# Two steps a unit and a fixed order for TensorE in one stage of a decoder kernel on Trainium2

## The chip, the cores and the metric

The kernel runs on one core of a Trainium2 chip (trn2). TensorE (PE in the profile) multiplies and transposes into PSUM; VectorE (DVE), ScalarE (ACT) and GpSimd (POOL) do the rest; SyncE (SP) issues most DMAs. The metric is the device time of one execution in microseconds (us), as the median of several runs. A profile comes from one execution of its own.

## The reference, cut to what matters

Two decoder layers run over eight sequences of 512 tokens of width 256, all in fp32. The stage in question is the self-attention of layer 1:

```
def _L1_attn_ref(x, wq, w_kv_down, w_k_up, w_v_up, wo):      # x: 8 x 512 x 256
    H, D = 16, 64
    q = heads(x @ wq.T)                                       # 8, 16, 512, 64
    kv_latent = x @ w_kv_down.T                               # width 128
    k = heads(kv_latent @ w_k_up.T)
    v = heads(kv_latent @ w_v_up.T)
    q = q * cos + rotate_half(q) * sin
    k = k * cos + rotate_half(k) * sin
    scores = einsum('bhsd,bhtd->bhst', q, k) / sqrt(D) + causal
    probs = softmax(scores)
    out = einsum('bhst,bhtd->bhsd', probs, v)
    return merged(out) @ wo.T
x = layernorm(x + _L1_attn_ref(x, ...))
```

Ahead of it stand layer 0's self-attention, a cross-attention and a feed-forward block; behind it a joint attention over the sequence and a context, and a mixture of experts.

## The kernel before, in words

The stage `l1_self` goes through 64 units: a unit is one sequence b (a "batch" below, of eight units) and one pair of heads c. The causal mask makes the rows of queries of unequal length, so a unit's four row blocks i are put in three groups: `GROUPS = ((0, 1), (2,), (3,))`, which need 128 + 256, 384 and 512 columns of scores. The helper `_pipeline` (L32) walks over (b, c, group) and calls, at each step, the stages of different units: `l1_pre` and `l1_scores` for the newest, `l1_transposes` two steps later (there is an empty stage between) and `l1_values` three steps later. After each step it runs one piece of work that was put off: half of a batch's output projection.

What each stage does:

- `l1_prepare` cuts the projections into pieces. `share` (once a batch) transposes x (L198) and makes the latents (L844). `q_and_k` makes queries (L852) and keys (L853) in one PSUM tile of the kind `s`; VectorE multiplies it by the cosines into `qk` (L857) and by the sines into `turned` (L858), and four DMAs on POOL's queue add `turned`, with halves of heads exchanged, into `qk` (L861). `v` makes the values (L868), which ScalarE copies (L870). The pieces lie in one list, `ahead`, and `l1_pre` takes one at two of the three steps of a unit.
- `l1_scores` multiplies queries by keys (L907) into an `s` tile; the two heads use half of the array's rows each. `masked_softmax` adds the mask and takes the maximum on VectorE in one instruction (L271), negates and scales the maximum (L281), and takes the exponential with its sum on ScalarE (L283). `scaled` divides by the sum on VectorE (L891, L893).
- `l1_transposes` turns the probabilities on TensorE (L939), three or four blocks into a PSUM tile of the kind `t`, and `evac` copies it to SBUF: in turn on VectorE (L108) and on ScalarE (L110).
- `l1_values` multiplies values by turned probabilities (L963) into an `o` tile; the two heads use half of the array's columns each. After a unit's last group, `out_done` copies the tile out; after a batch's last unit it puts off the output projection (`project_and_norm`: L239, then the sum and the layer norm on VectorE, L246 and L213 to L223, with one instruction on POOL, L216).

The program order is not the order of execution: a scheduler orders each engine's instructions at compile time by priority (the place in the program) and by when its own model thinks that operands and buffers are ready. In `l1_self` this holds for all engines. The next stage, `l1_context`, keeps TensorE in program order (`tc.manual_schedule(engines={PE})`). A tile that asks for a buffer in use makes its first writer wait.

[...] The setting `psum("b", 2, 2, 2)` gives two `s` tiles [...], two `t` tiles and two `o` tiles; `psum("c", 2, 3, 1)`, opened for the next stage, gives two, three and one. Under the latter, tiles made by `u_tile` come from `t`.

## Time and profile before

| What | Value |
|---|---|
| Median of 3 runs | 3648.78 us (3641.66 to 3656.81) |
| The profiled execution: its own time, its span | 3650.17 us, 3648.5 us |
| Busy share of the span: PE, DVE, ACT, POOL | 94%, 60%, 39%, 30% |
| Mean granted TensorE clock | 0.965 |
| Stage `l1_self`: first latents to last output projection | about 1257 to 2206 us |

A line of groups reads: line, engine, operation, tile written <- tiles read, shape, count, busy time and mean duration, and the idle time of the engine before it with what ended it. A line of waits reads: who waited <- for whom: us in total, times, longest. A line of stretches reads: from:to, length, busy time and count of PE, PEld, DVE, ACT and POOL, then the granted clock (1.00 is full), the share of the DMA engines, and GB/s. A line of the timeline reads: start, length, engine, line, operation, tiles, shape and count, and in brackets the idle time before it. A matrix product in fp32 leaves two records. For TensorE the first part of a shape, as 64*128, is the part of the array in use: rows and columns.

### The profile page before, as it was taken

Reading aid. Unit: us, or ns where it says so; the run is one execution under the profiler, and the core shown is the slowest. Engines: PE = TensorE matmul, PEld = TensorE weight load, DVE = VectorE, ACT = ScalarE, POOL = GpSimd, SP = SyncE. Lnnn points to the kernel's source line nnn. Section 1 sums busy time; section 2 is a strip of 40 time slices with the busy share of each in tenths; the row PEclk is TensorE's granted clock in tenths of the full one; section 3 lists DMA queues with packets and bytes.
Section 4 is the critical chain, followed back from the end, with each engine's and each line's share of the span. In section 5 each row is a group of like instructions: output and inputs, shape, how many; then the busy total and the mean of one; then the engine's idle time right before and its main releaser. Section 6 shows DMA issues by size and latency. Waiting matters only on the chain. (4 is left out here: it accounts for less than half of the span.)

```text
span 3648.5 us, 52874 instructions
## 1 busy us (share of the span) xinstructions
PE 3429.4 (94%) x19718; PEld 2117.7 (58%) x19718; DVE 2173.6 (60%) x6158; ACT 1437.9 (39%) x2947; POOL 1092.5 (30%) x960
## 2 busy tenths in 40 slices
PE   8999999998999899999999999999999998999995
PEld 3333343345666556665666666555555555888884
DVE  5776776656666377778777885665666655200112
ACT  2444444453434254445444553433333333222222
POOL 3877777762111122222222220010101101222222
PEclk8999999998999999999999999999999999999997
DMA  4000011110000297232222330000000002766674
GB/s 132 30 24 24 24 36 33 38 60 12 4 1 1 52 270 165 36 41 36 36 36 36 41 47 4 10 13 18 20 8 21 19 13 92 230 179 190 184 229 134
DMA packets 166002, 234.97 MB, mean 64 GB/s; under 512 B 26569, under 2 KB 128649, under 8 KB 165746
## 3 DMA queue, kind: packets, MB, share of 16 engines
q1 hardware_dynamic: 139010, 175.83, 15.8%
q0 software_dynamic: 25584, 51.57, 9.4%
q8 instruction: 156, 2.56, 0.3%
q10 hardware_dynamic: 1152, 4.19, 0.3%
q14 instruction: 100, 0.82, 0.1%
HBM read 135.83 MB, written 61.11 MB: 54 GB/s over the span
## 5 line engine op out<-in xcount | busy, mean ns | idle before, releaser
L430 DVE CUSTOM_DVE_ANT_0 scored<-s_sc,decay 128x512 f32<-128x512 f32 x512 | 323.5, 687 | 221.7 <-PE s_sc L425 220.6
L861 POOL DMA_DIRECT2D qk<-turned x256 | 202.9, 1205 | 657.0 <-PE t_v L868 264.9
L483 ACT ACTIVATE pt<-s_st 128x1024 f32<-128x1024 f32 x256 | 261.1, 1023 | 262.1 <-PE s_st L479 232.9
L283 ACT ACTIVATE p<-p,nm 128x128 f32<-128x128 f32 (+3 forms) x512 | 283.1, 554 | 159.7 <-DVE nm L281 157.0
L110 ACT COPY pt<-tP 128x512 f32<-128x512 f32 (+2 forms) x416 | 205.6, 496 | 308.4 <-PE tP L939 189.4
L1082 ACT ACTIVATE p<-s_sc,nm 128x576 f32<-128x576 f32 x256 | 191.1, 747 | 342.7 <-DVE nm L1081 241.3
L893 DVE TENSOR_SCALAR p<-p,rsum 128x576 f32<-128x576 f32 (+4 forms) x768 | 295.8, 427 | 5.5
L1439 DVE TENSOR_SCALAR y<-o_y,share 128x256 f32<-128x256 f32 x71 | 31.4, 479 | 397.2 <-PE o_y L1419 397.2
L1402 PE MATMUL s_h<-xnT,we 128*128 128x256 f32 (+1 forms) x1248 | 262.1, 364 | 0.6 <-DMA we<-in_mo_w 0.6
L1081 DVE TENSOR_REDUCE nm<-s_sc 128x1 f32<-128x576 f32 x256 | 185.2, 748 | 115.4 <-PE s_sc L1079 114.0
L1419 PE MATMUL o_y<-we,h 128*128 128x256 f32 x1136 | 251.4, 379 | 0.0
L271 DVE CUSTOM_DVE_ANT_0 p<-s_sc,tabs 128x128 f32<-128x128 f32 (+3 forms) x512 | 232.6, 482 | 16.5 <-PE s_sc L907 16.5
L108 DVE COPY pt<-tP 128x512 f32<-128x512 f32 (+2 forms) x416 | 235.9, 576 | 8.0 <-PE tP L1097 3.6
L1402 PEld LDWEIGHTS s_h<-xnT,we 128*128 128x128 f32 x1248 | 218.0, 192 | 25.5 <-DMA we<-in_mo_w 1.0
L1419 PEld LDWEIGHTS o_y<-we,h 128*128 128x128 f32 x1136 | 215.3, 190 | 29.0
L1440 POOL DMA_INDIRECT total<-y,to x71 | 110.2, 1553 | 397.8 <-DVE y L1439 181.7
L907 PE MATMUL s_sc<-qk 64*128 64x128 f32 (+3 forms) x1024 | 205.8, 474 | 14.3 <-DMA qk<-turned 12.7
L939 PEld LDWEIGHTS tP<-ident,p 128*128 128x128 f32 x1280 | 136.6, 140 | 126.2 <-issue 58.4
L939 PE MATMUL tP<-ident,p 128*128 128x128 f32 x1280 | 192.5, 283 | 11.8 <-DVE pt L108 8.0
L425 PE MATMUL s_sc<-k,q 32*128 32x512 f32 x1024 | 174.5, 671 | 25.8 <-ACT pt L483 23.2
L1245 POOL DMA_INDIRECT rows_in<-z,irow x64 | 62.8, 982 | 415.4 <-DVE hit L1240 304.8
L963 PE MATMUL o_pv<-pt,vc 128*64 128x128 f32 (+1 forms) x2304 | 184.2, 293 | 0.0
(282 smaller groups left out, 6566.4 us busy)
## 6 DMA issues: line engine op xcount, KB each, us to landing
we<-in_mo_w SPq DMA_DIRECT2D x78, 1024.0 KB, 5.7
rows_in<-zero SPq DMA_DIRECT2D x64, 530.0 KB, 12.8
qk<-turned POOLq DMA_DIRECT2D x256, 128.0 KB, 4.5
coef<-in_ff_upw SPq DMA_DIRECT2D x40, 256.0 KB, 3.2
coef<-in_ff_dnw SPq DMA_DIRECT2D x40, 256.0 KB, 3.2
xr<-rows_in SPq DMA_DIRECT2D x32, 265.0 KB, 6.4
x<-in_x SPq DMA_DIRECT2D x8, 512.0 KB, 9.8
total<-x SPq DMA_DIRECT2D x8, 512.0 KB, 2.9
```

The costliest lines, as they stand in the source:

```text
L108: dve.tensor_copy(dst, src)
L110: act.copy(dst, src)
L271: dve.tensor_tensor_reduce(out=p[:, j, 0:n], in0=s[:, j, 0:n], in1=m, scale=1.0, scalar=-3.0e38, op0=op, op1=reduced, accum_out=mx[:, j : ...
L283: act.activation(p[:, j, 0:n], p[:, j, 0:n], AF.Exp, bias=nm[:, j : j + 1], scale=scale, accum_out=sums[:, at + j : at + j + 1],)
L430: dve.tensor_tensor_reduce(out=scored[:, h, :], in0=s[:, j, :], in1=decay[:, i, :], scale=1.0, scalar=-3.0e38, op0=ALU.mult, op1=ALU.max, ...
L483: act.activation(pt, s, AF.Exp, scale=1.0 / 16.0)
L861: pool.dma_start(out=qk[h : h + 32], in_=other[g : g + 32], accum_op=ALU.add)
L893: dve.tensor_scalar(p[:, j, 0:n], p[:, j, 0:n], rsum[:, j : j + 1], None, ALU.mult)
L907: pe.matmul(s[:, j, at : at + n], lhsT=q[h : h + 64, i * P : (i + 1) * P], rhs=k[h : h + 64, 0:n], start=True, stop=True,)
L939: pe.transpose(t[:, n, :], p[:, j, at * P : (at + 1) * P], ident)
L1402: pe.matmul(s[:, j, :], lhsT=w1[:, c, f * P : (f + 1) * P], rhs=xnT[:, c, :], start=(c == 0), stop=(c == KC - 1),)
L1419: pe.matmul(o[:, i, :], lhsT=h[:, f, i * P : (i + 1) * P], rhs=w2[:, f, :], start=(f == 0), stop=(f == 7),)
```

## The change

1. A unit has two steps instead of three: group 0, then groups 1 and 2 together (`STEPS`). Each stage runs for all groups of its step. The transposes follow one step after the scores and the values two steps after, with no empty stage.
2. TensorE runs the stage in program order.
3. Queries and keys are projected two units ahead, with a third `qk` buffer; values one unit ahead. The transposes of x and the latents of the next batch are separate pieces at the two steps of unit 5. Before the loop come unit 0's pieces and unit 1's queries and keys.
4. In `masked_softmax` the VectorE instruction scales by -1/8 and takes the minimum, which gives the negated scaled maximum directly: the separate negation is gone, and the exponential's scale is -1.
5. The transposed probabilities are copied by ScalarE alone, into three buffers instead of two.
6. The PSUM setting `c` is opened before the stage instead of after it.

```diff
-    def masked_softmax(s, p, m, n, scale, add_or_mult, sums, at):
-
-        mx = col("mx", 2)
+    def masked_softmax(s, p, m, n, scale, sums, at):
+
         nm = col("nm", 2)
-        op, reduced = add_or_mult
         for j in range(2):
+
             dve.tensor_tensor_reduce(
                 out=p[:, j, 0:n],
                 in0=s[:, j, 0:n],
                 in1=m,
-                scale=1.0,
-                scalar=-3.0e38,
-                op0=op,
-                op1=reduced,
-                accum_out=mx[:, j : j + 1],
+                scale=-scale,
+                scalar=3.0e38,
+                op0=ALU.add,
+                op1=ALU.min,
+                accum_out=nm[:, j : j + 1],
             )
-        dve.tensor_scalar(nm, mx, -scale, None, ALU.mult)
         for j in range(2):
             act.activation(
                 p[:, j, 0:n], p[:, j, 0:n], AF.Exp,
-                bias=nm[:, j : j + 1], scale=scale, accum_out=sums[:, at + j : at + j + 1],
+                bias=nm[:, j : j + 1], scale=-1.0, accum_out=sums[:, at + j : at + j + 1],
             )
...
+    banks.close()
+    ctx.enter_context(psum("c", 2, 3, 1))
+
     def l1_prepare(b, c):
...
-        def share():
-            xT = x_transposed(b)
+        def turn():
+            live["xT", b] = x_transposed(b)
+
+        def latent():
+            xT = live["xT", b]
             latT = work.tile([P, S], F32, tag="lat", name="lat")
-            o = o_tile("o_lat")
+            o = u_tile("o_lat")
...
-            qk = ph.tile([P, 2, S], F32, tag="qk", name="qk", bufs=2)
+            qk = ph.tile([P, 2, S], F32, tag="qk", name="qk", bufs=3)
...
-        return ([share] if c == 0 else []) + [q_and_k, v]
-
-    ahead = [piece for b in range(NB) for c in range(8) for piece in l1_prepare(b, c)]
+        return ([turn, latent] if c == 0 else []) + [q_and_k, v]
+
+    units = [(b, c) for b in range(NB) for c in range(8)]
+    pieces_of = {u: l1_prepare(*u) for u in units}
 
     GROUPS = ((0, 1), (2,), (3,))
 
-    def l1_pre(b, c, m):
-
-        if (b, c, m) == (0, 0, 0):
-            for _ in range(3):
-                ahead.pop(0)()
-        if ahead and (m or c == 7):
-            ahead.pop(0)()
+    STEPS = ((0,), (1, 2))
+
+    def l1_pre(b, c, step):
+
+        at = units.index((b, c))
+        if step == 0 and at + 2 < len(units):
+            pieces_of[units[at + 2]].pop(-2)()
+        if step == 1 and at + 1 < len(units):
+            pieces_of[units[at + 1]].pop()()
+        if c == 5 and b + 1 < NB:
+            pieces_of[b + 1, 0].pop(0)()
...
+    def groups(stage):
+
+
+        def run(b, c, step):
+            for m in STEPS[step]:
+                stage(b, c, m)
+
+        return run
...
-        pt = pt_tile()
+        pt = pt_tile(bufs=3)
         order = [at for block in l1_blocks(m) for _, at in block]
         for j in range(2):
             t = t_tile("tP")
             for n, at in enumerate(order):
                 pe.transpose(t[:, n, :], p[:, j, at * P : (at + 1) * P], ident)
-            evac(pt[:, j, 0 : len(order), :], t[:, 0 : len(order), :])
+            act.copy(pt[:, j, 0 : len(order), :], t[:, 0 : len(order), :])
...
-    with phase("l1_self") as ph:
+    with phase("l1_self") as ph, tc.manual_schedule(engines={PE}):
+        for u, what in ((0, 0), (0, 0), (0, 0), (0, 0), (1, 0)):
+            pieces_of[units[u]].pop(what)()
         _pipeline(
-            [(b, c, m) for b in range(NB) for c in range(8) for m in range(len(GROUPS))],
-            [l1_pre, l1_scores, nothing, l1_transposes, l1_values],
+            [(b, c, step) for b in range(NB) for c in range(8) for step in range(len(STEPS))],
+            [
+                (0, groups(l1_scores)),
+                (0, l1_pre),
+                (1, groups(l1_transposes)),
+                (2, groups(l1_values)),
+            ],
             put_off,
         )
```

More of the change, by code (lines that the diff above doesn't have):

```diff
@@ L257, in p_tile, with pt_tile @@
         return ph.tile([P, 2, n], F32, tag="p", name="p", bufs=bufs)
-    def pt_tile():
-        return ph.tile([P, 2, NT, P], F32, tag="pt", name="pt")
+    def pt_tile(bufs=2):
+        return ph.tile([P, 2, NT, P], F32, tag="pt", name="pt", bufs=bufs)
     def col(name, n):
         return work.tile([P, n], F32, tag=name, name=name, bufs=4)
-    def masked_softmax(s, p, m, n, scale, add_or_mult, sums, at):
-        mx = col("mx", 2)
+    def masked_softmax(s, p, m, n, scale, sums, at):
         nm = col("nm", 2)
-        op, reduced = add_or_mult
         for j in range(2):
@@ L845, in share @@
             evac(latT, o)
-            live["xT", b], live["lat", b] = xT, latT
+            live["lat", b] = latT
         def q_and_k():
@@ L918, in l1_scores @@
             masked_softmax(
-                s[:, :, at : at + n], p[:, :, at : at + n], causal[:, S - n : S], n, 1.0 / 8.0, (ALU.add, ALU.max), sums, 2 * g
+                s[:, :, at : at + n], p[:, :, at : at + n], causal[:, S - n : S], n, 1.0 / 8.0, sums, 2 * g
             )
@@ L972, in l1_values @@
             out_done(b, c, live.pop(("o", b, c)), woT1, 8, lambda: xs[b])
-    with phase("l1_self") as ph:
+    with phase("l1_self") as ph, tc.manual_schedule(engines={PE}):
+        for u, what in ((0, 0), (0, 0), (0, 0), (0, 0), (1, 0)):
+            pieces_of[units[u]].pop(what)()
         _pipeline(
-            [(b, c, m) for b in range(NB) for c in range(8) for m in range(len(GROUPS))],
-            [l1_pre, l1_scores, nothing, l1_transposes, l1_values],
+            [(b, c, step) for b in range(NB) for c in range(8) for step in range(len(STEPS))],
[5 more added lines that the diff above has]
+            ],
             put_off,
         )
-    banks.close()
-    ctx.enter_context(psum("c", 2, 3, 1))
     q1_k1 = slot("q1_k1")
```

## The prediction

> **What bounds the kernel now.** I read the page's engine rows first, then the busy time in stretches, the waits inside the changed stage, and TensorE's order of time for one unit.

> ```profile
> span 3648.5 us, 52874 instructions
> PE 3429.4 (94%) x19718; PEld 2117.7 (58%) x19718; DVE 2173.6 (60%) x6158; ACT 1437.9 (39%) x2947; POOL 1092.5 (30%) x960
> ...
> 1268.00:1284.00 16.00, 8.27 (x19) 4.05 (x20) 5.24 (x25) 4.44 (x13) 4.30 (x6) 0.57 1.09 253
> 1400.00:2175.00 775.00, 761.46 (x5109) 480.09 (x5108) 617.30 (x2123) 374.14 (x1106) 183.06 (x225) 1.00 0.32 45
> 2222.00:2232.00 10.00, 8.52 (x35) 5.42 (x32) 6.84 (x13) 4.69 (x12) 0.00 (x0) 0.85 0.00 0
> ...
> PE s_sc L907 <- DMA qk<-turned: 12.7, 7, 8.3
> PE tP L939 <- DVE pt L108: 8.0, 9, 1.3
> ```

> The stage runs from about 1259 to 2206 us, 64 units. In 775 us of steady running TensorE is busy for 761.5 (98%), at full clock; its waits are small: 8.0 us for VectorE's copies of transposes, 12.7 for the DMAs of the turned queries, 8.3 of it in one wait at the start. A reader who stops here concludes that reordering can win 25 us at most. But a busy TensorE is not one at its peak, so I looked at one steady unit:

> ```profile
> 1599.98 1.98 PE L852 MATMUL s_q<-xT,wqT 128*128 128x512 f32 x4
> 1601.80 1.02 PE L853 MATMUL s_q<-lat,kd_ku 128*128 128x512 f32 x2
> 1602.75 0.93 PE L907 MATMUL s_sc<-qk 64*128 64x128 f32 x8
> 1603.61 0.88 PE L939 MATMUL tP<-ident,p 128*128 128x128 f32 x6
> 1604.41 0.87 PE L963 MATMUL o_pv<-pt,vc 128*64 128x256 f32 x8
> 1605.21 1.16 PE L868 MATMUL t_v<-vu,lat 128*128 128x128 f32 x8
> 1606.30 0.92 PE L907 MATMUL s_sc<-qk 64*128 64x384 f32 x4
> 1607.15 1.09 PE L939 MATMUL tP<-ident,p 128*128 128x128 f32 x8
> 1608.17 0.88 PE L963 MATMUL o_pv<-pt,vc 128*64 128x128 f32 x12
> 1608.98 1.13 PE L907 MATMUL s_sc<-qk 64*128 64x512 f32 x4
> 1610.04 0.87 PE L939 MATMUL tP<-ident,p 128*128 128x128 f32 x6
> 1610.84 1.09 PE L963 MATMUL o_pv<-pt,vc 128*64 128x128 f32 x16
> 1611.87 1.98 PE L852 MATMUL s_q<-xT,wqT 128*128 128x512 f32 x4
> ```

> The unit takes 11.89 us without a gap, yet it holds eleven changes of the array's shape (128*128, 64*128, 128*64). Their price can be read here. Eight transposes take 1.02 us (1607.15 to 1608.17), six take 0.80: 0.11 each, so about 0.14 of a run belongs to no transpose. Sixteen value products take 1.03, twelve 0.81: 0.055 each, 0.15 of the run fixed. Scores of 512 columns take 1.06, of 384 take 0.85: 0.21 per 128 columns, about 0.2 fixed. Starts in the trace show the same: the last transpose before value products holds its place for 202 ns instead of 109; the first pair of value projections after value products takes 213 instead of 112, after an output projection (same shape) 109. Between runs of one shape nothing is lost: from latents (L844) to transposes the interval is the plain 429.

> **The change part by part.**

> *TensorE's order.* Now a unit has eleven runs: three of transposes (0.15 with entry and exit), three of value products (0.15), three of scores (0.19), the query/key projection (0.20), the value projection (0.20): 1.87 us. In two steps the order is: scores of group 0; queries/keys, then the earlier unit's transposes of groups 1 and 2 (one shape, no change between); value products of group 0; scores of groups 1 and 2 in one run; value projection, then transposes of group 0 (one shape); value products of groups 1 and 2. Six runs: 0.19 + 0.20 + 0.15 + 0.19 + 0.20 + 0.15 = 1.08. Saved: 0.79 us a unit, 6.3 a batch of eight. Each of two output projections a batch now stands between value products and scores instead of before a projection of its own shape: 0.2 more each, 0.4.

> *A steady batch now* takes 116.1 us (first query projections at 1483.55 and 2063.90, five batches apart). Its work without stalls: 8 x 11.89 + 64 output-projection records x 0.216 (13.8) + eight transposes of x at 0.109 and four latent records at 0.429 (2.6) + 0.3 of changes = 111.8. So 4.3 are stalls: one transpose wait of about 1.1 behind the norm, about 0.18 in most units, small ones. Nearly all are transposes waiting for VectorE's copy with two PSUM buffers. The change gives three, and the copy to ScalarE, which answers both.

> *New batch:* 116.1 - 4.3 - 6.3 + 0.4 = 105.9 if nothing stalls.

> *VectorE.* Out go 256 negations (L281, 42.6 us busy) and half of the copies of transposes (70.0 + 42.4). These overlap their neighbours, so I count 130: of 732 busy in the stage some 600 remain, 69% of a stage of 870. The mask-and-maximum instruction keeps its shape; a min for a max and another scale cost nothing extra that I can see (bounded by 10 ns on 683 either way, 5 us hidden).

> *ScalarE.* In come 128 copies of 384 columns at 470 ns and 63 of 512 at 568: 96 us, 447 to 543, 62%. Cover for them is TensorE; I place them by hand in a unit of 11.1 us from its first scores. Group 0's scores end at 0.85, queries/keys at 3.5, transposes of groups 1 and 2 at 5.0, value products at 5.9, scores 1 and 2 at 6.7 and 7.6, values at 8.7, transposes 0 at 9.3, value products at 11.1. VectorE masks group 1 from 6.9 and group 2 until 9.0 (0.48 and 0.61 a head from start to start); ScalarE's exponentials (about 0.6 and 0.7 a head with the read of the sum) end at 8.7 and 10.1, with the three copies ahead of them 11.3; the scaling ends at 12.4. The transposes that wait for it stand at 14.6 and 15.3: slack 2.9. Thinnest is the scores' PSUM (two buffers): scores 2 at 6.7 need the buffer of the queries/keys, which VectorE empties in two instructions of 1.14 from 3.7 at the earliest: 6.0 to 6.5. I charge 0.15 a unit, 1.2 a batch (bounds 0 and 0.9 a unit).

> *The norm*, once a batch, holds VectorE for 4.4 us (L246 to L223, a wait of 1.2 for POOL in it) just after 6.9 us of output projection; in a fixed order TensorE cannot pass it. Group 1's masks may wait 4.4, and the next scores and queries/keys want those buffers 4 us later. I take 1.5, between 0 and 4.4, near the 1.1 to 1.3 of today's waits.

> *Rule against row, evacuation.* The row: ScalarE copies 384 columns in 470 ns where VectorE takes 547, and it idles half of the stage. [...] TensorE makes four tiles in 1.5 us, ScalarE empties them in about 1.7 alone, and the fourth needs the first's buffer. [...] by the row the first copy is done 0.1 before it is needed unless an exponential stands ahead. I go with the row.

> *Rule against row, clock.* Half clock followed the 8.3 us wait (0.57 in 1268 to 1284), but also a wait of 1.5 us near 2227 (0.85 in the ten us around); waits of 1.3 in the steady stage left 1.00. [...] by the row at 2227 it could cost 3.4 us at half clock, 1.7 more, 14 over eight batches. I leave it out and keep it for the range.

> *DMAs and queues.* The four DMAs a unit (POOL, 4.5 us median to land) are the same, two units ahead: the small waits for them in the first batch (2.4 us in all) go. They pass no other work on POOL but the norm's power, which waits at most for one issue group. SP issues nothing new. The opening wait of 8.3 stays: units 0 and 1 are still projected, then scores wait for the first landing at about 1275.6, and the clock falls as now. The third query/key buffer and the third pt buffer only take space. Opening the new PSUM pools earlier moves a change of pools from the end to the start of the stage; I cost it at nothing (bounds -1 and +2). The drain, with nothing left to project, loses about 1.

> **Sum.** A batch: 105.9 + 1.2 + 1.5 = 108.6, 7.5 less than now; seven of them 52.5. The first batch, without output projection: 6.3 + 2.4 less about 2.7 for filling and the slow clock, 6. Drain -1. Together 57 or 58. The profiled execution took 3650.17 (span 3648.5), 1.4 above the median of the runs, 3648.78: 3592 on the median's scale.

> **The rivals.**

> *The fixed order makes VectorE the pacemaker (slower).* Place: the PSUM buffer of queries/keys, needed by scores 2. If VectorE's queue puts both scalings of group 0 (1.3 us) and that of group 2 (1.0) ahead of emptying it, the buffer comes at 8.3 instead of 6.0, 1.7 us late in each unit: 109 us lost against 57, 3700. The gain is gone from 0.9 us a unit, and slower by half a per cent from 1.2. For it: VectorE is the fullest engine after TensorE, and in the next stage, whose order is also fixed, TensorE idles 7% of 2230 to 3030. Against: 130 us of VectorE's work leave here, and half of that idling is six waits of up to 5.6 us for L1039, once a batch, which the norm's term above covers. 9%.

> *The gain halves.* Late copies on ScalarE, or the norm's stall with the clock behind it, take 0.3 to 0.6 a unit: 20 to 40 us are left, 3609 to 3629. 20%.

> *The change of shape is not what costs,* and only idle time goes: 4.3 - 2.7 a batch, about 13 us in all, 3636. Against it stand the equal-shape intervals above. 9%.

> *More than expected:* no stalls, 10.2 x 7 + 8 = 79: 3569. Within the likeliest case's edge.

> **Chances.** The likeliest case (gain 40 to 80) 62%; halved 20%; no change 9%; slower 9%. Half a per cent, 18 us, is about what a measurement of this kernel tells from no change. Faster by more 0.82, within 0.09, slower 0.09. Range 3564 to 3630; the likeliest alone 3569 to 3609.

> **What would show it.** Right: steady batches of 107 to 110 us; s_q followed by tP without a 0.09 step, s_sc of groups 1 and 2 back to back; VectorE near 600 us and ScalarE near 540 in the stage; DMA waits of scores only at the start. Wrong: TensorE idle before s_sc L907 for VectorE's L858, or before tP for ScalarE, more than 0.5 us a unit; PEclk below 1.00 in the middle of the stage; transposes that still pay 0.05 on entry after a projection.

## The result, and the profile after

The changed kernel takes 3597.78 us (median of 4 runs, 3590.26 to 3602.03); the kernel before, run beside it, 3652.8 (4 runs, 3641.66 to 3665.78). The ratio is 0.9846, 95% interval 0.9827 to 0.9866: faster by 55 us, 1.5%. The forecast was 3592 from 3648.78, 57 us.

The page's engine rows of the changed kernel, and its busy time in stretches that answer to the opening and the steady middle of before:

```profile
span 3600.3 us, 52648 instructions
PE 3374.1 (94%) x19718; PEld 2124.2 (59%) x19718; DVE 2080.9 (58%) x5710; ACT 1504.2 (42%) x3139; POOL 1097.2 (30%) x960
```

```profile
1280.00:1296.00 16.00, 7.54 (x16) 3.33 (x16) 2.91 (x10) 1.86 (x8) 5.16 (x7) 0.57 1.09 274
1400.00:2125.00 725.00, 706.17 (x5023) 479.36 (x5022) 526.39 (x1721) 422.48 (x1246) 182.33 (x221) 1.00 0.35 53
```

TensorE has the same 19718 instructions and the same busy share, 94%, in a span 48 us shorter. In the middle it is idle for 18.8 of 725 us (2.6%), a little more than before (13.5 of 775, 1.7%): idle time is not what went. The opening is as slow as before, clock 0.57. One steady unit in TensorE's order of time shows what went:

```profile
1596.34 1.98 PE L856 MATMUL s_q<-xT,wqT 128*128 128x512 f32 x4
1598.16 1.02 PE L857 MATMUL s_q<-lat,kd_ku 128*128 128x512 f32 x2
1599.02 1.77 PE L957 MATMUL tP<-ident,p 128*128 128x128 f32 x14
1600.72 0.87 PE L981 MATMUL o_pv<-pt,vc 128*64 128x256 f32 x8
1601.52 1.77 PE L925 MATMUL s_sc<-qk 64*128 64x384 f32 x8
1603.22 1.16 PE L872 MATMUL t_v<-vu,lat 128*128 128x128 f32 x8
1604.22 0.82 PE L957 MATMUL tP<-ident,p 128*128 128x128 f32 x6
1604.97 1.75 PE L981 MATMUL o_pv<-pt,vc 128*64 128x128 f32 x28
1606.65 0.93 PE L925 MATMUL s_sc<-qk 64*128 64x128 f32 x8
1607.50 0.70 PE L856 MATMUL s_q<-xT,wqT 128*128 128x512 f32 x1
```

The same products, now 11.16 us from one s_q to the next, in six runs of one array shape: fourteen transposes take 1.77 where eight and six took 1.09 and 0.87 in runs of their own, 28 value products 1.75 where 16 and 12 took 1.09 and 0.88, and the scores of groups 1 and 2 stand back to back. Over the stage the runs of one shape fall from 725 to 400.

TensorE's waits inside the stage after the change:

```profile
PE s_q L856 <- DVE nm L270: 12.2, 7, 2.9
PE s_sc L925 <- DMA qk<-turned: 9.1, 2, 8.2
PE tP L957 <- ACT pt L958: 4.5, 11, 0.9
PE s_sc L925 <- DVE turned L862: 3.7, 7, 1.8
PE o_lat L848 <- DVE xT L108: 1.6, 1, 1.6
```

The wait for VectorE's copies (8.0) has become one of 4.5 for ScalarE's. New is the first row: once a batch the query projection waits for the mask behind the norm. The scores wait for the turned queries only at the start.

Parts of the stage, from the first latents to the last output projection (us):

| | before | after | gain | forecast |
|---|---|---|---|---|
| first latents to first scores | 18.0 | 16.2 | 1.8 | 0 |
| first scores of unit 0 to those of unit 8 | 104.8 | 96.7 | 8.1 | 6 |
| unit 8 to unit 63 | 796.0 | 752.0 | 44.0 | 52.5, with the last batch |
| from there to the end | 29.7 | 26.9 | 2.8 | -1 |
| stage | 948.5 | 891.8 | 56.7 | 57 to 58 |
| a steady batch | 116.1 | 109.6 | 6.5 | 7.5 |

The two profiled executions differ by 48.1 (3650.17 and 3602.03), because the stage began 13.7 us later in the second, with TensorE's order before it unchanged; behind the stage 5.1 us were won. Such starts lay between 1255.3 and 1275.9 us in the fourteen profiled executions of this study, not in step with what a kernel changed. The time at half clock (a granted clock of 0.50) ahead of the stage lay between 116 and 160 us: 116.1 in before, 146.8 in after. By an estimate from the granted 0.50, half of the difference is lost by it, up to 22 us and 15.4 between these two, so the clock can account for the spread of the starts. So the parts below are compared by the length of the stage, and the whole by the ratio of the runs.

### The profile page after: what moved, and what is told of

It is laid out like the page before. It is cut to its first block, busy times and chain, and to the rows that moved or that the text cites. A ratio compares the mean times of both kernels' runs of the same rounds, so it can differ in the third digit from the quotient of the medians.

```text
span 3600.3 us, 52648 instructions
## 1 busy us (share of the span) xinstructions
PE 3374.1 (94%) x19718; PEld 2124.2 (59%) x19718; DVE 2080.9 (58%) x5710; ACT 1504.2 (42%) x3139; POOL 1097.2 (30%) x960
## 5 line engine op out<-in xcount | busy, mean ns | idle before, releaser
L281 ACT ACTIVATE p<-p,nm 128x128 f32<-128x128 f32 (+3 forms) x512 | 282.5, 553 | 301.3 <-DVE nm L270 300.0
L902 DVE TENSOR_SCALAR p<-p,rsum 128x576 f32<-128x576 f32 (+4 forms) x768 | 300.1, 432 | 9.8
L270 DVE CUSTOM_DVE_ANT_0 p<-s_sc,tabs 128x128 f32<-128x128 f32 (+3 forms) x512 | 225.1, 483 | 55.8 <-PE s_sc L925 55.7
L423 PE MATMUL s_sc<-k,q 32*128 32x512 f32 x1024 | 175.2, 674 | 26.8 <-ACT pt L481 23.2
L958 ACT COPY pt<-tP 128x384 f32<-128x384 f32 (+1 forms) x384 | 172.9, 513 | 44.6 <-PE tP L957 44.1
L925 PE MATMUL s_sc<-qk 64*128 64x128 f32 (+3 forms) x1024 | 176.8, 460 | 12.8 <-DMA qk<-turned 9.1
L1120 PE MATMUL tP<-ident,p 128*128 128x128 f32 x1024 | 143.5, 282 | 40.4 <-DVE k L1062 25.1
L957 PE MATMUL tP<-ident,p 128*128 128x128 f32 x1280 | 169.4, 276 | 5.8 <-ACT pt L958 4.5
L957 PEld LDWEIGHTS tP<-ident,p 128*128 128x128 f32 x1280 | 144.7, 141 | 49.7 <-issue 28.0
L981 PE MATMUL o_pv<-pt,vc 128*64 128x128 f32 (+1 forms) x2304 | 167.5, 290 | 0.0
```

The costliest lines, as they stand in the source:

```text
L270: dve.tensor_tensor_reduce(out=p[:, j, 0:n], in0=s[:, j, 0:n], in1=m, scale=-scale, scalar=3.0e38, op0=ALU.add, op1=ALU.min, accum_out=nm[ ...
L281: act.activation(p[:, j, 0:n], p[:, j, 0:n], AF.Exp, bias=nm[:, j : j + 1], scale=-1.0, accum_out=sums[:, at + j : at + j + 1],)
L902: dve.tensor_scalar(p[:, j, 0:n], p[:, j, 0:n], rsum[:, j : j + 1], None, ALU.mult)
L957: pe.transpose(t[:, n, :], p[:, j, at * P : (at + 1) * P], ident)
L1120: pe.transpose(t[:, k, :], p[:, (S + P) * j + k * P : (S + P) * j + (k + 1) * P], ident)
```

## The experiments

Line numbers move by a few between the kernels; names of tiles are the same. "Stage", "batch" and "unit" are as above; after is 891.8, 109.6 and 11.16. Each edit is made in the changed kernel unless it says otherwise.

### Is it the changes of shape?

**Values between the scores.** The value projection is put between the scores of groups 1 and 2, so that two more runs of one shape stand in each unit; everything else stays.

```diff
+    def scores_and_pre(b, c, step):
+        l1_scores(b, c, step)
+        l1_pre(b, c, step)
+        if step == 1:
+            l1_scores(b, c, 2)
...
-                (0, groups(l1_scores)),
-                (0, l1_pre),
+                (0, scores_and_pre),
```

> The changed kernel with one move: in a unit's second step the value projection stands between the scores of group 1 and those of group 2, so scores are two runs and the transposes of group 0 follow scores instead of a projection. The instructions are the same. Theory A (a change of the array's shape costs 0.15 to 0.2 us a run): runs 0.19 + 0.20 + 0.19 + 0.15 in place of 0.19 + 0.20, so 0.34 more a unit, 11.50 for a steady unit instead of 11.16, and about 22 us more for the stage than the changed kernel's 891.8 (first latents to the last output projection), time near 3620. Theory B (only waits cost, a shape change is free): unit 11.16 and the stage within 4 us of 891.8.

Measured: stage 909.2, batch 111.8, 526 runs of one shape, 3612.82 us, ratio to before 0.9869 (0.9842 to 0.9895). Its steady unit, TensorE's order of time:

```profile
1603.48 0.92 PE L925 MATMUL s_sc<-qk 64*128 64x384 f32 x4
1604.33 1.16 PE L872 MATMUL t_v<-vu,lat 128*128 128x128 f32 x8
1605.42 1.13 PE L925 MATMUL s_sc<-qk 64*128 64x512 f32 x4
1606.48 0.88 PE L957 MATMUL tP<-ident,p 128*128 128x128 f32 x6
```

The unit is 11.52: 0.36 more for two runs, where 0.34 was expected. The stage is 17.4 us longer for 126 more runs, 0.14 each, with no operation added. TensorE's idle time (the stage less its busy time) fell meanwhile from 30.9 to 26.8 us, and half clock rose from 20.5 to 23.9, worth 1.7 at the granted 0.50; without both, a run costs 0.16, and in the dense unit 0.18.

**Three steps, in a fixed order.** Groups 1 and 2 get a step each again; fixed order, lookahead, copies and mask are the new ones.

```diff
-    STEPS = ((0,), (1, 2))
+    STEPS = ((0,), (1,), (2,))
...
-        if c == 5 and b + 1 < NB:
+        if c == 5 and b + 1 < NB and step < 2:
...
-                (1, groups(l1_transposes)),
-                (2, groups(l1_values)),
+                (2, groups(l1_transposes)),
+                (3, groups(l1_values)),
```

> The changed kernel with a unit in three steps again, one group each; TensorE's order stays fixed, transposes two steps and values three steps after the scores, queries/keys still two units ahead. Nine runs of one shape a unit (three of scores, three of value products, queries/keys with transposes, values with transposes, transposes alone) instead of six. Theory A: 1.57 instead of 1.08 us of shape changes, so 0.49 more a unit: 11.65 a steady unit, stage 891.8 + 31 = 923, time near 3629. Theory B: no dearer than the changed kernel, as each softmax has more time and only one group's burst at a time: stage 885 to 892.

Measured: 593 runs, the unit 11.59, but stage 900.0 and 3600.35 us, 0.9837 (0.9807 to 0.9866). The 193 runs at 0.14 are 27 us; the stage lost 8.2. Most of the difference comes back as shorter waits: idle time falls from 30.9 to 17.5 us (the wait behind the norm from 12.2 to 4.5), and half clock from 20.5 us to 13.7, worth 3.4. Whether the more even work of three steps does that, or the longer way from the scores to the transposes, was not separated. So the two steps pay for their fewer changes of shape with longer waits once a batch. In the time of the runs this kernel and the change can't be told apart.

Read against the kernel before, this run says one thing more. It has only 132 runs of one shape fewer, some 19 us, and its stage is 48.5 us shorter. Some 20 of the other 29 are waits of the old order: idle time fell from 26.7 to 17.5, and the late copies that made half of the old units 0.33 longer are gone. Fewer changes of shape are one way to the gain and not the only one.

**TensorE's order left to the scheduler.**

```diff
-    with phase("l1_self") as ph, tc.manual_schedule(engines={PE}):
+    with phase("l1_self") as ph:
```

> The changed kernel without the fixed order of TensorE: the scheduler orders it by its own model. The program asks for the same six runs, and the scheduler departs from them in some 17 places of the stage. Theory A: a departure splits a run and costs 0.3 to 0.4, but lets TensorE pass the waits behind the norm (1.1 us a batch): stage between 885 and 900. If the fixed order itself is what brings the gain: stage above 920.

Measured: stage 891.0, unit 11.16, 424 runs, 3592.3 us, 0.9824 (0.9788 to 0.9859). Given the two steps, the scheduler finds almost the same order. With them, fixing the order is worth nothing more.

### What keeps the new order fed?

**One unit ahead.** Queries and keys are projected one unit ahead, with two buffers.

```diff
-        if step == 0 and at + 2 < len(units):
-            pieces_of[units[at + 2]].pop(-2)()
+        if step == 0 and at + 1 < len(units):
+            pieces_of[units[at + 1]].pop(-2)()
...
-            qk = ph.tile([P, 2, S], F32, tag="qk", name="qk", bufs=3)
+            qk = ph.tile([P, 2, S], F32, tag="qk", name="qk", bufs=2)
...
-        for u, what in ((0, 0), (0, 0), (0, 0), (0, 0), (1, 0)):
+        for u, what in ((0, 0), (0, 0), (0, 0), (0, 0)):
```

> The changed kernel with queries and keys projected one unit ahead (two qk buffers) at the same place of the step. Keys end 3.5 us after a unit's first scores, VectorE's two multiplications end near 6.3, the four DMAs are issued by about 8 and land 4.5 later: 12 to 13, where the next scores stand at 11.16. Theory: TensorE waits 1 to 2 us in each unit for DMA qk<-turned, stage 950 to 1020, half clock more often. If the landing is hidden anyway (the lookahead is idle): stage within 4 us of 891.8.

Measured: stage 1052.5, 3751.82 us (two runs), 1.0282 (1.0251 to 1.0313). Its waits of TensorE in the stage:

```profile
PE s_sc L925 <- DMA qk<-turned: 109.3, 75, 10.6
PE s_q L856 <- DVE nm L270: 12.5, 7, 2.9
```

In a fixed order TensorE has nothing else to do while the turned queries travel, and 109 us at half clock (20.5 in after) add another 44. The second unit of lookahead, with its buffer, is a condition of the change as it stands: without it the stage is 161 us longer. Whether a free order would fill these waits was not tried.

**The negation put back.** The mask takes the maximum, a second instruction scales and negates it; the rest is the change.

```diff
-                scale=-scale,
-                scalar=3.0e38,
+                scale=1.0,
+                scalar=-3.0e38,
                 op0=ALU.add,
-                op1=ALU.min,
-                accum_out=nm[:, j : j + 1],
+                op1=ALU.max,
+                accum_out=mx[:, j : j + 1],
             )
+        dve.tensor_scalar(nm, mx, -scale, None, ALU.mult)
...
-                bias=nm[:, j : j + 1], scale=-1.0, accum_out=sums[:, at + j : at + j + 1],
+                bias=nm[:, j : j + 1], scale=scale, accum_out=sums[:, at + j : at + j + 1],
```

> The changed kernel with the separate negation of the maxima on VectorE (256 instructions of 128x2, 160 ns, about 70 from start to start). If it lay beside other work in the steady unit, as the prediction's hand-placed unit says: unit stays 11.16, only the stall behind the norm grows by 0.1 to 0.3 a batch, stage 891 to 896. If VectorE is nearly the pacemaker: 0.07 x 4 = 0.28 a unit, stage 910.

Measured: stage 924.4, batch 113.7, 3629.88 us, 0.9944 (0.9918 to 0.9969). An instruction of 0.16 us, 256 of them, costs 32.6 us of the stage, though VectorE's busy time in it rises only from 636 to 653 us of 924. Of the 32.6, 22.5 are idle time of TensorE (53.4 instead of 30.9) and 6.8 its slower work in 13.6 us more of half clock. The wait of TensorE in the stage that grew, and one such stall in the timeline (this kernel's L271, L283, L858, L904, L959 and L960 are the changed kernel's L270, L281, L856, L902, L957 and L958; L281 is the negation):

```profile
PE tP L959 <- ACT pt L960: 29.7, 40, 2.1
```

```profile
1721.37 1.98 PE L858 MATMUL s_q<-xT,wqT 128*128 128x512 f32 x4
1721.91 0.87 DVE L904 TENSOR_SCALAR p<-p,rsum 128x512 f32<-128x512 f32 x2
1722.70 0.28 DVE L271 CUSTOM_DVE_ANT_0 p<-s_sc,tabs 128x128 f32<-128x128 f32 x1
1723.46 0.16 DVE L281 TENSOR_SCALAR nm<-mx 128x2 f32<-128x2 f32 x1
1723.66 0.40 ACT L283 ACTIVATE p<-p,nm 128x128 f32<-128x128 f32 x1 [2.09 <-DVE nm L281]
1724.05 1.25 PE L959 MATMUL tP<-ident,p 128*128 128x128 f32 x10
1725.43 1.80 ACT L960 COPY pt<-tP 128x384 f32<-128x384 f32 x4
1725.94 0.66 PE L959 MATMUL tP<-ident,p 128*128 128x128 f32 x4 [0.63 <-ACT pt L960]
```

The same place in the changed kernel:

```profile
1596.34 1.98 PE L856 MATMUL s_q<-xT,wqT 128*128 128x512 f32 x4
1596.45 0.29 DVE L270 CUSTOM_DVE_ANT_0 p<-s_sc,tabs 128x128 f32<-128x128 f32 x1 [0.22 <-PE s_sc L925]
1596.79 0.40 ACT L281 ACTIVATE p<-p,nm 128x128 f32<-128x128 f32 x1 [0.45 <-DVE nm L270]
1599.02 1.77 PE L957 MATMUL tP<-ident,p 128*128 128x128 f32 x14
1599.60 1.84 ACT L958 COPY pt<-tP 128x384 f32<-128x384 f32 x4 [0.95 <-PE tP L957]
```

Without the negation ScalarE starts as soon as the first head's minimum is out, is done with group 0 before the transposes, and waits 0.95 us for them. With it, the first exponential needs both heads' maxima and one more instruction, and ScalarE still exponentiates when the transposes come; its copies wait in its queue, and the fourth tile of transposes waits for the first copy. From the start of s_q (medians over all units but the first two): the first exponential starts at 1.87 instead of 0.65 us, the last of group 0 ends at 3.74 instead of 2.51, and the transposes start at 2.68 in both. Of the 1.22 later start, 0.58 lies between mask and exponential, and 0.64 is inherited: the mask itself is late, since the scalings of the group before (L904), which waited for their own exponentials, stand ahead of it in VectorE's queue.

**The negation taken out of the kernel before, alone.** The same edit, reversed, in the old order.

```diff
-                scale=1.0,
-                scalar=-3.0e38,
-                op0=op,
-                op1=reduced,
-                accum_out=mx[:, j : j + 1],
+                scale=-scale,
+                scalar=3.0e38,
+                op0=ALU.add,
+                op1=ALU.min,
+                accum_out=nm[:, j : j + 1],
             )
-        dve.tensor_scalar(nm, mx, -scale, None, ALU.mult)
...
-                bias=nm[:, j : j + 1], scale=scale, accum_out=sums[:, at + j : at + j + 1],
+                bias=nm[:, j : j + 1], scale=-1.0, accum_out=sums[:, at + j : at + j + 1],
```

> The kernel before, with the negation of the row maxima alone taken out (the change's form of the masked softmax); order, shapes, copies and projections as before. Putting the negation back into the changed kernel lengthened the stage by 32.6 us and gave tP waits for ScalarE's copies of 29.7 us. Theory A, the negation's place in the chain matters only where all transposes of two groups follow each other and their copies queue on ScalarE behind late exponentials: here the copies are shared with VectorE and groups come one at a time, so the stage stays within 946 to 950 us of before's 948.5, the time 3646 to 3656. Theory B, the chain of one unit is a price of its own wherever it stands: 20 to 33 us of the stage go here too, the time 3620 to 3633. In both VectorE falls by 20 to 40 us of busy time over the stage and the half clock stays near 14 us.

Measured: stage 946.2 (before 948.5), 3653.66 us, 0.9999 (0.9986 to 1.0011). As theory A said, the edit is worth nothing in the old order, and 32.6 us in the new one. That shared copies and single groups are the reason follows from the traces above, and was not tried by itself. VectorE's busy time fell by 3 us (736 to 733), not by the 20 to 40 that both theories expected: the records of the negation, 0.166 each and 42.6 together, overlap those of its neighbours (in before one of 0.16 starts at 1599.02, the next instruction at 1599.08).

**The copies shared again.** In the changed kernel the turned probabilities are copied in turn on VectorE and ScalarE.

```diff
-            act.copy(pt[:, j, 0 : len(order), :], t[:, 0 : len(order), :])
+            evac(pt[:, j, 0 : len(order), :], t[:, 0 : len(order), :])
```

> The changed kernel with the copies of transposed probabilities in turn on VectorE and ScalarE again, all else kept. Theory of the prediction (ScalarE has room, VectorE is the fuller engine): VectorE gets about 95 us of work back and the waits for it behind the norm and for the scores' buffers grow by 0.1 to 0.5 us a unit: stage 900 to 925. [...]

Measured: stage 909.1, unit 11.49 in most, 3611.24 us, 0.9876 (0.984 to 0.9912). The waits of TensorE in the stage that changed:

```profile
PE tP L957 <- ACT pt L110: 13.1, 42, 0.7
```

One such wait in the timeline:

```profile
1722.06 1.25 PE L957 MATMUL tP<-ident,p 128*128 128x128 f32 x10
1722.97 0.48 ACT L110 COPY pt<-tP 128x384 f32<-128x384 f32 x1 [1.06 <-PE tP L957]
1723.50 0.66 PE L957 MATMUL tP<-ident,p 128*128 128x128 f32 x4 [0.19 <-ACT pt L110]
1724.94 1.15 DVE L108 COPY pt<-tP 128x384 f32<-128x384 f32 x2
```

VectorE is busy for 726 us instead of 636, and the copy of the first tile stands in its queue behind the two multiplications of 1.14 to 1.22 us that empty the query/key buffer just then; it begins at 1724.94. The fourth tile of transposes does not wait for that: it starts at 1723.50, as ScalarE's copy of the second tile ends (1722.97 + 0.48). So it seems to take the second tile's buffer, which is full three transposes, 3 x 0.11 = 0.33 us, later than the first's. By that much most units are longer.

**ScalarE's copies in the kernel before.** Only the copies, three buffers for them and the PSUM setting are taken over; order, negation and lookahead are the old ones.

```diff
-            evac(pt[:, j, 0 : len(order), :], t[:, 0 : len(order), :])
+            act.copy(pt[:, j, 0 : len(order), :], t[:, 0 : len(order), :])
...
-        pt = pt_tile()
+        pt = pt_tile(bufs=3)
...
-            o = o_tile("o_lat")
+            o = u_tile("o_lat")
...
+    banks.close()
+    ctx.enter_context(psum("c", 2, 3, 1))
+
     def l1_prepare(b, c):
```

> The kernel before with one part of the change alone: transposed probabilities are copied by ScalarE only, into three buffers, and the PSUM setting with three t tiles and one o tile is opened before the stage. Three steps and TensorE's free order as before. Theory: the waits of transposes for VectorE's copies go (11.4 us in the stage, and the small ones of 0.18 in most units), the array's shape changes stay near 725: unit 11.9 instead of 12.2, stage 948.5 less 15 to 30: 918 to 933. Theory B (waits are all that the change removed): stage near 895.

Measured: stage 953.6, 3659.57 us, 1.0012 (0.9998 to 1.0027). The transposes no longer wait; the scores do:

```profile
PE s_sc L910 <- DVE turned L861: 20.5, 26, 2.1
PE s_sc L910 <- DMA qk<-turned: 15.3, 9, 7.5
```

The waits for copies, 8.0 us in before, came back as others in the old order. This edit moved PSUM and copies together; which of the two makes the new wait was not separated.

### What is left of the stalls?

**GpSimd's addition kept in its place.** The scheduler had moved the next stage's addition of a bias (L1144, GpSimd) into this one in the first two batches. The changed kernel's timeline at the first norm:

```profile
1418.51 1.03 POOL L216 TENSOR_TENSOR rs<-ve,mhalf 128x4 f32<-128x4 f32 x1 [5.50 <-DVE ve L215]
1419.58 1.38 DVE L223 TENSOR_SCALAR x<-r,mv,rs 128x256 f32<-128x256 f32 x4 [1.16 <-POOL rs L216]
1421.05 2.36 POOL L1144 TENSOR_TENSOR xb<-x,bo 128x1024 f32<-128x1024 f32 x1 [1.50 <-DVE rsum L900]
1421.55 2.40 DVE L902 TENSOR_SCALAR p<-p,rsum 128x384 f32<-128x384 f32 x2
1424.61 3.10 PE L856 MATMUL s_q<-xT,wqT 128*128 128x512 f32 x4 [2.87 <-DVE nm L270]
```

Two scalings of 384 columns take 2.40 us beside that addition; elsewhere such a pair takes 0.75. TensorE waits 2.87 and 2.93 us in these two batches and 1.28 in the five others.

```diff
-            pool.tensor_tensor(xb, xs[b], bo1.unsqueeze(1).to_broadcast([P, NT, D]), ALU.add)
+            tc.keep_in_program_order(
+                pool.tensor_tensor(xb, xs[b], bo1.unsqueeze(1).to_broadcast([P, NT, D]), ALU.add)
+            )
```

> The changed kernel with the next stage's addition of its bias to x on POOL (the tile xb, 128x1024, 2.35 us) kept in POOL's program order, so that it no longer runs inside this stage, where two of them stand beside a VectorE scaling that takes 2.06 us in place of 0.42. Theory [...]: the two waits of queries/keys of 2.87 us fall to the 1.2 of the other batches and the half clock after one of them goes: stage 891.8 - 3.3 - 1.7, 886 to 889. Rival (the long scaling has another cause): the 2.06 us scaling is still there, stage 891.

Measured: stage 890.4, 3599.6 us, 0.9862 (0.9838 to 0.9885). Only the second batch's addition left the stage, and with it the long scaling and the long wait: 1.29 us there instead of 2.93, and 10.6 behind all norms instead of 12.2. The first batch kept all three. So the addition is the cause, as the theory said. How it holds VectorE up, the traces show in part: the first of the two scalings starts 0.5 us after the addition, takes 2.07 us where 0.42 is usual, and ends 0.2 us after the addition's end; that looks like waiting for the addition, not like running slowly beside it. In the time of the runs nothing can be seen.

**The norm's scaling on ScalarE.**

```diff
-                normed(xs[b], r)
+                normed(xs[b], r, on_act=n == 8)
```

> The changed kernel with the last part of the layer 1 norm behind each batch (the scaling of the four row tiles) on ScalarE in place of VectorE. Theory A, TensorE's wait for the mask instruction behind the norm (1.1 us in six batches, 2.87 us in two, 12.2 in all) is VectorE's queue: it falls to under 4 us in all, the stage to 882 to 887 us, time 3588 to 3593. Theory B, the wait moves to ScalarE: the norm's instructions stand before copies of tP or exponentials and tP waits for the copies rise from 4.8 to 10 us or more; stage 889 to 897 us, time 3595 to 3603.

Measured: stage 888.1, 3587.43 us (3577.08 to 3599.88), 0.9805 (0.9777 to 0.9834). The waits of TensorE in the stage:

```profile
PE tP L957 <- ACT pt L958: 12.8, 12, 2.0
PE s_sc L925 <- DMA qk<-turned: 9.8, 2, 9.0
```

The mechanism is theory B's, with less loss than it named: the 12.2 us behind the norm are gone, and the transposes' waits for ScalarE rise by about 8. The wait changed its engine; 3.7 us of the stage remain as a gain. The median fell by more than the stage explains, with an interval that overlaps the change's.

**The fills held back.** The zero fills of the routed rows on SyncE's queue wait for unit 0's queries.

```diff
-    for n in range(NE * REGION // (NT * P)):
-        sp.dma_start(out=fills[n], in_=zero.unsqueeze(1).to_broadcast([P, NT, ROW]))
...
+        dve.tensor_scalar(zero[:, 0:1], live["qkv", 0, 0][0][:, 0:1], 0.0, None, ALU.mult)
+        for n in range(NE * REGION // (NT * P)):
+            sp.dma_start(out=fills[n], in_=zero.unsqueeze(1).to_broadcast([P, NT, ROW]))
```

> The changed kernel with the zero fills of the routed rows, which SyncE's queue writes beside the beginning of the stage, held back until the first unit's turned queries and keys have landed. Theory A, the opening wait of the scores for that transfer (8.2 us in the changed kernel) is contention with the fills: it falls to 2 to 4 us, and the half clock at the start with it, stage 891.8 to 882 to 887, time 3588 to 3593. Theory B, the wait is the transfer's own latency from its issue and the fills don't matter: wait 7 to 8.5 us, stage 889 to 893, time 3595 to 3600. Against both stands that the fills now lie beside the following units' transfers: with two units of lookahead (22 us) I expect no wait of scores from that; if there is one, the time is up to 10 us longer.

Measured: stage 886.6, first latents to first scores 12.2 instead of 16.2, 3592.78 us, 0.9834 (0.9808 to 0.9861). TensorE's first two waits and the stretch of the opening:

```profile
1279.05 0.76 PE L923 MATMUL s_sc<-qk 64*128 64x128 f32 x2 [4.19 <-DMA qk<-turned]
1281.35 1.61 PE L923 MATMUL s_sc<-qk 64*128 64x128 f32 x6 [1.54 <-DMA qk<-turned]
```

```profile
1276.00:1292.00 16.00, 9.60 (x36) 5.10 (x36) 7.86 (x26) 3.15 (x13) 7.19 (x10) 0.79 0.99 202
```

Half of the opening wait of 8.21 us was contention with the fills (theory A; the wait is just above what it named), and half clock in the stage fell from 20.5 to 13.7 us. The first eight transfers land in 5.2 us (median) instead of 8.6. What the other 4.2 us of the wait consist of was not separated.

**The three together.** The edits of the last three kernels in one.

> The changed kernel with three edits together: the addition of the next stage's bias on GpSimd kept in the program's order, the zero fills behind the first unit's queries, and the layer 1 norm's scaling on ScalarE. Alone they made the stage 890.4, 886.6 and 888.1 us against 891.8. If the gains add (they lie at different places: two batches' norms for the first, the opening for the second, eight norms for the third, which overlaps with the first by up to 1.4), the stage is 881 to 884 us and the time 3584 to 3590. If the waits only change hands, with the fills beside the first batch and the norm's instructions beside ScalarE's copies, the stage is 886 us or more and the time 3591 or more.

Measured: stage 881.8, 3589.09 us, 0.9825 (0.9794 to 0.9856). In the stage the gains add (1.4 + 5.2 + 3.7 = 10.3 of 891.8; measured 10.0). The runs can't tell it from the change: 0.9825 lies inside the interval of 0.9846. It has the shortest stage, and is not shown to be the faster kernel.

## Why the prediction was right, and where it was off

**The bound.** Right: TensorE's 98% in the middle was not its peak, and changes of array shape were the price. The unit was to fall from 11.89 to 11.10 and fell to 11.16: 0.73 of the 0.79. The two experiments that put runs of one shape back give the price: the dense units, 11.52 with two more runs and 11.59 with three, say 0.18 and 0.14 for each. The dense units account for 64 x 0.73 = 47 of the 56.7 us, which is 325 runs at 0.14. The start and the drain gave 4.6. The other 5 are an estimate from the batches' waits: four units of eight took 12.22 before, 0.33 above the dense one for late copies (10.6 us over the stage, where the prediction had read 0.18 in most units), and the new waits behind the norm took about half of that back. That three steps reach a stage of 900.0 with 593 runs shows that the waits were a second way to much of this gain; the prediction put all that idle time could give at about 13 us.

**The steady batch.** 109.6 for 108.6, inside the 107 to 110 named. The missing 1.0 a batch is 0.5 from the unit (8 x 0.06), 0.3 from the unit with the next batch's transposes of x and latents (3.2 us more than a plain one, 2.9 charged), and 0.3 from the two long waits; the stalls charged at 2.7 came to about 2.5 in the other batches. Over the stage that term was 8 us too large, and the first batch (8.1 for 6), the start (1.8 for 0) and the drain (2.8 for -1) gave it back. The right total is partly luck.

**The norm.** Charged 1.5 a batch, measured 1.28 in five and 2.9 in two. The long ones are not the norm's alone, but the addition on GpSimd beside it, which the prediction had not seen in the stage. On the clock: after the wait of 2.87 it was at half for 3.41 us (0.83 in 1421 to 1431), after that of 2.93 it stayed at 1.00 (1533 to 1543), after 1.28 too (1640 to 1650). So half clock can follow a wait of this length, as the row at 2227 had said (1.48 us of wait, then 3.41 at half clock from 2228.97), but need not; it cost 1.7 us once, an estimate from 3.41 us at the granted 0.50, not 14.

**Evacuation.** The row was right in the new order: with shared copies the stage is 17.3 us longer (909.1 for 891.8). But "the first copy is done 0.1 before it is needed unless an exponential stands ahead" hung on a step that the prediction did not price: the negation decides whether one does.

**The negation.** This is the term that was mis-sized. It stood in the sum only as VectorE's relief, 42.6 us of busy time, hidden; the hand-placed unit took the exponentials' place as given, with a slack of 2.9. Alone in the old order it is indeed worth nothing (0.9999), and little of its busy time was ever there: 3 us fell away with it in the old order, 17 came back in the new. In the new order it is 32.6 us: more than half of the gain hangs on it, because it brings the exponentials out of the way of the copies. That the forecast total came out is luck in this part: it took the unit without stalls for granted; without this edit it would have been "the gain halves" at its edge (3629.88).

**The lookahead.** Sized at 2.4 us in the first batch, from the waits that the old order had. The right question was what the fixed order would wait for without it: 161 us.

**The fixed order.** Nothing was charged for it alone, and with two steps it is worth nothing. VectorE did not become the pacemaker: the scores wait for L862 3.7 us in the whole stage, where 1.2 a batch was charged.

**What was to be seen.** No step between s_q and tP, scores back to back, DMA waits of scores only at the start: as named. VectorE 636 us for "near 600", ScalarE 515 for "near 540": records overlap, so taking an instruction out moves less busy time than its mean says (3 us for the 42.6 of the negations in the old order). The opening wait of 8.3 stayed (8.2). In the new order the new pools cost nothing that shows.

## What to carry to other kernels

Where a TensorE that is never idle changes its array shape often, group the work by shape: here 0.14 to 0.18 us for each run saved, some forty of them a batch. Weigh it against the waits that larger groups bring: the stage with three steps and 593 runs was 8 us longer than that with two and 400. Once the order is dense, price each small instruction by the place where it stands in the chain that comes round again each unit, mask, exponential, scaling, next mask, and by what queues behind the late engine; not by its busy time. Ask of each part both what it brings alone and what the rest is worth without it: here the copies and the negation brought nothing alone, and the whole loses 17 to 161 us without any one of the copies, the negation or the lookahead.
